# Value products one slot later, in front of a 512-column query product, and key fetches a pair ahead

## The chip, the cores and the metric

The kernel runs on one core of a Trainium2 chip. The metric is the device time of one execution in microseconds. The comparison of interest is between the kernel before the change and the kernel after it.

The engines are called by the names of the profile: PE is TensorE (matmuls), PEld its weight loads, DVE is VectorE, ACT is ScalarE, POOL is GpSimd, and SP is SyncE, which issues nearly all DMAs here. Each engine runs its instructions in the order in which the program gives them.

## The reference

The input is 16 sequences of 256 positions with 256 features. Two layers are computed, each as `x = x + s * silu(f)`, where `s` and `f` both read the layer norm `xn` of `x`. In layer 0 `s` is a linear recurrence and `f` a feed-forward block. The change lies in layer 1, where `s` is causal attention with 16 heads over a compressed key and value of 64 features, and `f` a linear layer with low-rank experts:

```python
q = concat([q_nope, apply_rope(q_rope)])            # per head 128 + 64
c_kv = rms_norm(x @ Wkv_a[:, :64]) * kv_norm_w      # 64 features, shared by the heads
k, v = from c_kv @ Wkv_b ; k gets the rotated shared 64 features as well
scores = where(causal, q @ k.T / sqrt(192), -inf)   # 256 x 256 per head and sequence
out = softmax(scores) @ v @ Wo
```

## The kernel before, in words

The 4096 tokens are worked on in 8 chunks of 512 tokens, that is of two sequences ("batches" b = 0 and 1 of the chunk). Layer 0 fills the first 283 us or so. After that comes the main loop of layer 1, written out by hand: 64 units, with loop variable `i`. A unit is one batch of one group of four heads in one chunk: `ch, r = divmod(i, 8)`, so a chunk has eight slots r = 0 to 7, and b is 0 in even slots and 1 in odd ones. Units 2n and 2n+1 form pair n, which has one chunk and one group of four heads. There are 32 pairs.

All engines are wrapped by a helper (`InOrder`, line 53) that ties each instruction to the one before it on its engine, so the program's order is the order on each engine, and nearly every line of the profile shows L53. Instructions are therefore told apart by their tiles.

What a slot `i` of the loop does, in the order on TensorE:

- `score_pack(u, 0)`: scores (`sc`) of the blocks with 256 and 224 keys. Behind it VectorE adds the mask and takes the maxima (`nm`), ScalarE takes the exponentials into `pr` and sums them (`sr`).
- `query_mm`: a product of 512 columns (`pq`) for the queries of a later pair, number 3 in an even slot, number 0 in an odd slot.
- `score_pack(u, 1)`: the blocks with 192, 160 and 128 keys.
- in an odd slot `query_mm(n, 1)`, another `pq`, and on VectorE `query_mul` (`qmul`).
- `turn(w, ...)` and `send(w)` for the unit before, `w`: VectorE transposes the normalised `pr` in 32x32 blocks into `turned`, and four DMAs on SyncE write it to a DRAM buffer `far`.
- in an even slot from the sixth on, `values_of(n)` for the pair that ended two slots earlier: 16 products of 64x64 weights, seen as 32 records, from `pT` into two PSUM banks `av`, and two copies on ScalarE to `attT`.
- `score_pack(u, 2)`: the blocks with 96, 64 and 32 keys; in an odd slot then `query_mm(n, 2)`, the second `query_mul`, and on GpSimd `query_rot`, which writes `qrot`.
- extra work of the chunk in certain slots: the gate in r = 0 and 1, the transposes `tp` of the next chunk's `xn` in r = 2 (`transpose_chunk`; `xn` is written by VectorE in the same slot, `norm_end`), the keys in r = 4, the router in r = 6, and the output product (`fast_end`) in r = 3, 4, 5 and 7.

`values_of(n)` reads two tiles, `pT[0]` and `pT[1]`, one for each half of the keys. Each has 128 partitions, 64 for each batch. They are filled by `fetch(n, y, b)`: one DMA on SyncE from `far[b]` into `pT[y]`, 384 KB. So a pair needs four fetches, and the products run through the first key half before the second:

```python
for z in (0, 2, 1, 3):
    ...
    heads = q.pT[z % 2][:, :, c0 : c0 + S - n0].rearrange("p (a hh) q -> p a hh q", hh=2)
```

The ring of `pT` has three buffers, that of `far` two, the small PSUM ring (tag `m1`: `pq`, `av`, `tp`, `pg`, `pkv` and others) five, the ring of `sc` three. In an even slot SyncE also issues `query_move`: eight DMAs from `qrot` into `qg`, the queries of a later pair.

The order of fetches before: in even slot 2n+2 `fetch(n, 0, 0)` at the start and `fetch(n, 1, 0)` behind `send`; in odd slot 2n+3 `fetch(n, 0, 1)` and `fetch(n, 1, 1)`, both at the start.

Of the kernel before, what the change touches and what calls it, by code (L numbers as in the profile page):

```python
# [41 lines left out]
def tile_two_layers(ctx: ExitStack, tc: tile.TileContext, d: dict, out: bass.AP):  # L42
# [181 lines left out]
    def m1(name, shape):  # L224
        return place["pool"].tile(shape, F32, tag=place["tag"], name=name)
# [204 lines left out]
    def query_move(n):  # L430
        q = groups[n]
        for r in range(2):
            for h in range(G):
                sp.dma_start(
                    q.qg[64 + 32 * r : 96 + 32 * r, :, h, :],
                    q.rot[32 * h : 32 * h + 32, r, :].rearrange("p (a q) -> p a q", q=32),
                )
# [892 lines left out]
    def gate_end(ch, jp):  # L1330
        k = chunks[ch]
        g = k.g2[:, 2 * jp : 2 * jp + 2, :]
        ve.scalar_tensor_tensor(g, g, 1.0, k.h, ALU.add, ALU.mult)
# [31 lines left out]
    def score_pack(u, pi):  # L1365
        k, b, pack = chunks[u.ch], u.b, PACK[pi]
        if pi == 0:
            u.nm = sm1.tile([P, NQ], F32, tag="nm", name=f"nm_{u.n}", bufs=3)
            u.sr = sm1.tile([P, NQ], F32, tag="sr", name=f"sr_{u.n}", bufs=3)
        qg = groups[u.i // 2].qg  # L1370
        sc = ps_sc.tile([P, CH], F32, tag="sc", name=f"sc_{u.n}_{pi}")
        for a, o in pack:
            pe.matmul(
                sc[:, o : o + 32 * (a + 1)], qg[:, b * NQ + a, :, :].rearrange("p h q -> p (h q)"),
                k.kT[:, b * S : b * S + 32 * (a + 1)], start=True, stop=True,
            )
        ends = [o + 32 * (a + 1) for a, o in pack]
        step = ends[1] - ends[0]
        n = len(pack)
        assert ends == [ends[0] + step * z for z in range(n)]  # L1380
        if ends[0] - 32 + step * n <= CH:
            diag = sc[:, ends[0] - 32 : ends[0] - 32 + step * n].rearrange("p (n s) -> p n s", n=n)[:, :, 0:32]
        else:
            diag = sc[:, ends[0] - step : ends[-1]].rearrange("p (n s) -> p n s", n=n)[:, :, step - 32 : step]
        ve.tensor_tensor(diag, diag, bc(kmask, n), ALU.add)
        for a, o in pack:
            ve.tensor_reduce(
                u.nm[:, a : a + 1], sc[:, o : o + 32 * (a + 1)], AX.X, ALU.max, negate=True
            )
        for a, o in pack:  # L1390
            w = 32 * (a + 1)
            ac.activation(
                u.pr[:, OFF[a] : OFF[a] + w], sc[:, o : o + w], AF.Exp,
                bias=u.nm[:, a : a + 1], accum_out=u.sr[:, a : a + 1],
            )

    def normalise(u, packs):
        blocks = [a for pi in packs for a, _ in PACK[pi]]
        lo, hi = min(blocks), max(blocks) + 1
        ve.reciprocal(u.sr[:, lo:hi], u.sr[:, lo:hi])  # L1400
        for a in blocks:
            v = u.pr[:, OFF[a] : OFF[a] + 32 * (a + 1)]
            gp.tensor_scalar(v, v, u.sr[:, a : a + 1], 1.0, ALU.mult, ALU.mult)
# [32 lines left out]
    def fetch(n, y, b):  # L1436

        q = groups[n]
        if y == b == 0:
            q.pT = {}  # L1440
        if b == 0:
            q.pT[y] = pp.tile([P, G, 3 * P], F32, tag="pT", name=f"pT_{n}_{y}", bufs=3)
        sp.dma_start(
            q.pT[y][64 * b : 64 * b + 64].rearrange("p h q -> p (h q)"),
            q.far[b].rearrange("(y k) s h z q -> y (k s) (h z q)", y=2)[y],
        )
# [35 lines left out]
    def values_of(n):  # L1482

        q = groups[n]
        ch, g = divmod(n, NG)
        k = chunks[ch]
        av = [m1(f"av_{ch}_{g}_{b}", [P, 2, S]) for b in range(2)]
        for z in (0, 2, 1, 3):
            n0 = 64 * z
            c0 = (0, 64, S, S + 64)[z]  # L1490
            heads = q.pT[z % 2][:, :, c0 : c0 + S - n0].rearrange("p (a hh) q -> p a hh q", hh=2)
            for b in range(2):
                rows = slice(64 * b, 64 * b + 64)
                for hh in range(2):
                    pe.matmul(
                        av[b][64 * hh : 64 * hh + 64, :, n0:S], k.rowv[rows, z, :],
                        heads[rows, :, hh, :], start=(z == 0), stop=(z == 3),
                    )
        k.attT.append(a2.tile([P, 2, CH], F32, tag="attT", name=f"attT_{ch}_{g}", bufs=6))
        for b in range(2):  # L1500
            ac.copy(k.attT[g][:, :, b * S : (b + 1) * S], av[b])
# [27 lines left out]
    def out_weights(i):  # L1529
        if i == PER:  # L1530
            gp.tensor_tensor(TO[1], wo(0, 1), wo(0, 0), ALU.subtract)
            gp.tensor_tensor(TO[2], wo(1, 1), TO[1], ALU.subtract)
        elif i == PER + 2:
            gp.tensor_tensor(TO[4], TO[2], wo(1, 0), ALU.subtract)
        elif i == PER + 4:
            gp.tensor_tensor(TO[3], wo(1, 1), wo(0, 1), ALU.subtract)
        elif i == 2 * PER + 1:
            TO[4] = X[0].rearrange("p j (n s) -> p (j n) s", s=DH)[:, 0:KP]
            gp.tensor_tensor(TO[4], TO[2], wo(1, 0), ALU.subtract)
# [105 lines left out]
    for i in range(LAST):  # L1645
        ch, r = divmod(i, PER)
        odd = i % 2 == 1
        u, w = units[i], units[i - 1] if i else None
        here = w is not None and w.i >= LAST - 2
        n = (i + 3) // 2 if odd else (i + 2) // 2  # L1650
        n = n if n < len(groups) else None
        more = ch + 1 < NCH
        last = ch - 1 if ch == NCH - 1 and r in FINISH else None
        fast = ch - 1 if 0 < ch < NCH - 1 else None

        if not odd and n is not None:
            query_move(n)
        if odd and i > 2:
            fetch((i - 3) // 2, 0, 1)
            fetch((i - 3) // 2, 1, 1)  # L1660
        elif i and not odd:
            fetch((i - 2) // 2, 0, 0)
        score_pack(u, 0)
        if w:
            normalise(w, (2,))
        if fast is not None and r > 3:
            fast_begin(fast, r)
        if ch > 1 and r == 0:
            fast_begin(ch - 2, 0)
        out_weights(i)  # L1670
        if r == 1:
            gate_end(ch, 0)
        if r == 2:
            gate_end(ch, 1)
            if more and ch:
                norm_end(ch + 1)
        if r == 5 and more:
            kv_end(ch + 1)
        if i == LAST - 1:

            finish_mm(last, 3, 0, NPAIR)
            finish_out(last, 3)
            last = None
        if w:
            for z in (1, 2):
                turn_here(w, z) if here else turn(w, z)

        if r == 0:
            mid_chunk(ch)
        if r == 7 and more:  # L1690
            key_chunk(ch + 1)
        if n is not None:
            query_mm(n, 0 if odd else 3)
            if not odd:
                query_lat(n, 3)
        if i == 5:
            values_of(0)
        score_pack(u, 1)

        if odd and n is not None:  # L1700
            query_mm(n, 1)
            query_mul(n, 0)
        if w:
            if here:
                turn_here(w, 0)
            else:
                turn(w, 0)
                send(w)
        if not odd:
            if i > 4:  # L1710
                values_of((i - 4) // 2)
            if i:
                fetch((i - 2) // 2, 1, 0)
        score_pack(u, 2)
        normalise(u, (0, 1))

        if odd and n is not None:
            query_mm(n, 2)
            query_mul(n, 1)
            query_rot(n)  # L1720
            query_lat(n, 2)
        if r < 2:
            gate_begin(ch, r)
        if r == 0 and more and ch:
            norm_begin(ch + 1)
        if r == 2 and more:
            transpose_chunk(ch + 1)
        if r == 4 and more:
            kv_begin(ch + 1)
        if r == 6 and more:  # L1730
            router_chunk(ch + 1)
        if last is not None:
            j = FINISH.index(r)
            finish_mm(last, j, 0, NPAIR)
            finish_out(last, j)
        if fast is not None and r in FINISH:
            fast_end(fast, r)
# [94 lines left out]
```

## Time and profile before

| | |
|---|---|
| median of 3 runs | 909.54 us (907.01 to 910.27) |
| profiled execution | 908.09 us, span 906.3 us |
| granted TensorE clock, mean | 0.996 |
| TensorE busy | 894.5 us (99%), 5426 matmuls |
| VectorE, GpSimd, ScalarE busy | 664.7 us (73%), 570.2 us (63%), 475.3 us (52%) |
| value products `av` | 992 records, 80.2 us busy |
| score products `sc` | 1024 records, 175.2 us busy |
| query products `pq` | 512 records, 122.6 + 120.2 us busy |
| fetches `pT<-far` | 124 DMAs of 384 KB, median 4.9 us to landing |
| sends `far<-turned` | 248 DMAs of 192 KB, median 4.3 us to landing |
| moves `qg<-qrot` | 256 DMAs of 64 KB, median 2.8 us to landing |

The span is the time from the first to the last recorded instruction. Busy times add up the records of an engine and count overlapping time once. A matmul's record overlaps with its neighbours, as matmuls are pipelined, so the distance from one start to the next says more than a record's duration. In a timeline, records of the same shape that follow each other are joined, and the first column is the start of the first in microseconds from the start of the span. A bracket names the wait ahead of a record and what ended it.

### The profile page before, as it was taken

The numbers are of one execution on the slowest core, as the hardware profiler recorded it, in microseconds if no ns is written. First come the engines' busy times: TensorE is split into PE (matmuls) and PEld (weight loads), VectorE is DVE, ScalarE is ACT, GpSimd is POOL, SyncE is SP. The second block draws the span as 40 slices with busy tenths as digits, with TensorE's granted clock in tenths as the row PEclk, the third lists the DMA queues.
The fourth block names the chain that finished last, engine by engine and source line by source line (L and its number), as shares of the span: only waits on it lengthen the run. The fifth ranks groups of instructions, "written<-read, shape, count | busy, mean of one in ns | idle before, by whom it ended". The sixth has DMA issues, their size and how long they took to land.

```text
span 906.3 us, 17455 instructions
## 1 busy us (share of the span) xinstructions
PE 894.5 (99%) x5426; PEld 670.2 (74%) x5426; DVE 664.7 (73%) x2017; ACT 475.3 (52%) x1562; POOL 570.2 (63%) x885
## 2 busy tenths in 40 slices
PE   8999999999999999999999999999999999999998
PEld 7768899987767656777677677767767776776776
DVE  6876687665587879668967876896787689678662
ACT  3235556564336646555554664555466456546541
POOL 1228787878345537687586768648776864876541
PEclk9999999999999999999999999999999999999999
DMA  9730000000013887877987887788788778878881
GB/s 282 237 116 2 1 2 1 1 1 2 0 24 75 201 226 172 216 175 180 226 195 176 195 205 178 181 223 209 163 215 189 178 185 224 205 163 219 192 246 35
DMA packets 197404, 134.00 MB, mean 148 GB/s; under 512 B 143104, under 2 KB 187968, under 8 KB 197312
## 3 DMA queue, kind: packets, MB, share of 16 engines
q1 hardware_dynamic: 195184, 128.69, 57.7%
q0 software_dynamic: 1152, 3.67, 1.2%
q8 instruction: 44, 0.72, 0.3%
q10 hardware_dynamic: 976, 0.53, 0.2%
q14 instruction: 48, 0.39, 0.1%
HBM read 63.11 MB, written 52.95 MB: 128 GB/s over the span
## 4 chain that ended last, share of the span: by engine, by line
PE 89%; DMA 4%; SPq 3%; DVE 2%; POOL 1%; issue 0%; ACT 0%; POOLq 0%; ACTq 0%
PE pq L53 21%; PE sc L53 14%; PE po L53 10%; PE av L53 7%; PE r L53 7%; PE f L53 7%; PE ph L53 5%; PE pf L53 5%; PE pg L53 4%; SPq L53 3%; DMA far<-turned 2%; PE pm L53 2%; DMA pT<-far 2%; PE tp L53 2%; PE pkv L53 1%; PE py L53 1%
## 5 line engine op out<-in xcount | busy, mean ns | idle before, releaser
L53 POOL TENSOR_SCALAR pr<-pr,sr 128x256 f32<-128x256 f32 (+7 forms) x512 | 191.6, 393 | 186.7 <-DVE sr L53 181.2
L53 ACT ACTIVATE pr<-sc,nm 128x256 f32<-128x256 f32 (+7 forms) x512 | 189.8, 381 | 218.8 <-DVE sr L53 140.8
L53 PEld LDWEIGHTS sc<-kT,qg 128*128 128x128 f32 x1024 | 157.5, 190 | 54.5 <-issue 40.7
L53 PE MATMUL sc<-kT,qg 128*128 128x256 f32 (+7 forms) x1024 | 175.2, 305 | 0.0
L53 DVE TENSOR_REDUCE nm<-sc 128x1 f32<-128x256 f32 (+7 forms) x512 | 127.6, 301 | 6.6
L53 DVE STREAM_TRANSPOSE turned<-pr 128x512 f32<-128x512 f32 x186 | 123.2, 687 | 10.9 <-POOL pr L53 10.1
L53 PE MATMUL pq<-xnT,wlat 128*128 128x512 f32 x256 | 122.6, 602 | 0.0
L53 PE MATMUL pq<-xnT,wrope 128*128 128x512 f32 x256 | 120.2, 593 | 0.0
L53 ACT ACTIVATION_READ_ACCUMULATOR pr<-sc,nm 128x1 f32 x512 | 104.1, 203 | 0.0
L53 DVE TENSOR_TENSOR sc<-sc,kmask 128x96 f32<-128x96 f32 (+1 forms) x192 | 45.4, 236 | 54.9 <-PE sc L53 53.6
L53 POOL TENSOR_TENSOR qrot<-qmul,qmul 128x512 f32<-128x512 f32 x64 | 83.4, 1323 | 2.8 <-DVE qmul L53 2.8
L53 PE MATMUL av<-pT,rowv 64*64 64x512 f32 (+2 forms) x992 | 80.2, 442 | 4.0 <-DMA pT<-far 3.6
L53 DVE TENSOR_TENSOR qmul<-pq,rot_q 128x512 f32<-128x512 f32 x128 | 80.7, 672 | 0.1
L53 ACT ACTIVATE qg<-pq 64x512 f32<-64x512 f32 x128 | 75.4, 589 | 4.3 <-PE pq L53 3.5
L53 PEld LDWEIGHTS av<-pT,rowv 64*64 64x64 f32 x992 | 37.5, 134 | 43.8 <-issue 31.7
L53 PEld LDWEIGHTS pq<-xnT,wrope 128*128 128x128 f32 x256 | 45.7, 191 | 32.4 <-issue 32.1
L53 PEld LDWEIGHTS pq<-xnT,wlat 128*128 128x128 f32 x256 | 45.7, 191 | 31.6 <-issue 31.6
L53 PEld LDWEIGHTS po<-wout,attT 128*128 128x128 f32 x416 | 58.4, 191 | 9.4 <-issue 4.0
L53 PE MATMUL po<-wout,attT 128*128 128x128 f32 (+1 forms) x416 | 64.2, 308 | 0.0
L53 POOL TENSOR_TENSOR rs<-ve,mhalf 128x4 f32<-128x4 f32 (+1 forms) x17 | 16.8, 986 | 48.6 <-DVE ve L53 34.6
L53 PE MATMUL ph<-xnT,p1T 128*128 128x256 f32 (+1 forms) x128 | 44.3, 503 | 0.8 <-DVE xnT L53 0.8
L53 POOL TENSOR_TENSOR attT<-attT,attT 128x512 f32<-128x512 f32 x36 | 45.1, 1273 | 0.0
(229 smaller groups left out, 1518.7 us busy)
## 6 DMA issues: line engine op xcount, KB each, us to landing
far<-turned SPq DMA_DIRECT2D x248, 192.0 KB, 4.3
pT<-far SPq DMA_DIRECT2D x124, 384.0 KB, 4.9
qg<-qrot SPq DMA_DIRECT2D x256, 64.0 KB, 2.8
x<-in_x_dram SPq DMA_DIRECT2D x7, 512.0 KB, 9.2
out_dram<-x POOLq DMA_DIRECT2D x12, 256.0 KB, 3.5
wqn_wo<-in_wq_nopeT_dram SPq DMA_DIRECT2D x4, 512.0 KB, 4.7
wqn_wo<-in_Wo_dram SPq DMA_DIRECT2D x4, 512.0 KB, 5.7
p2T<-in_proj2T_dram SPq DMA_DIRECT2D x2, 512.0 KB, 8.3
```

What stands on the lines that cost most here:

```text
L53: r = getattr(self.engine, name)(*args, **kw)
```

## The change

The products of pair n move from even slot 2n+4, behind `send` and ahead of `score_pack(u, 2)`, to odd slot 2n+5, behind `score_pack(u, 1)` and ahead of `query_mm(n, 1)`. Pair 0, which was in slot 5 ahead of `score_pack(u, 1)`, is now behind it. The two fetches of the second key half both go into odd slot 2n+3, behind `send` of unit 2n+2. The first fetch of the first half stays at the start of the even slot and the second at the start of the odd slot. The products of the last two pairs, after the loop, keep their place. Every instruction of before is still there, with the same shape.

```diff
         if odd and i > 2:
             fetch((i - 3) // 2, 0, 1)
-            fetch((i - 3) // 2, 1, 1)
         elif i and not odd:
             fetch((i - 2) // 2, 0, 0)
         score_pack(u, 0)
...
-        if i == 5:
-            values_of(0)
         score_pack(u, 1)
 
+        if odd and i > 4:
+            values_of((i - 5) // 2)
         if odd and n is not None:
             query_mm(n, 1)
             query_mul(n, 0)
...
                 turn(w, 0)
                 send(w)
-        if not odd:
-            if i > 4:
-                values_of((i - 4) // 2)
-            if i:
-                fetch((i - 2) // 2, 1, 0)
+        if odd and i > 2:
+            fetch((i - 3) // 2, 1, 0)
+            fetch((i - 3) // 2, 1, 1)
         score_pack(u, 2)
         normalise(u, (0, 1))
```

In the even slots TensorE's order becomes pack 0, `pq`, pack 1, pack 2, extra work. In the odd slots it becomes pack 0, `pq`, pack 1, the products, `pq`, pack 2, `pq`, extra work. ScalarE's two copies to `attT` move with the products.

## The prediction

> **What bounds the kernel now.** I read the profile page first: engine totals, the 40 slices, the chain that ended last, the groups.
>
> ```profile
> PE 894.5 (99%) x5426; PEld 670.2 (74%) x5426; DVE 664.7 (73%) x2017; ACT 475.3 (52%) x1562; POOL 570.2 (63%) x885
> PE   8999999999999999999999999999999999999998
> PE 89%; DMA 4%; SPq 3%; DVE 2%; POOL 1%; issue 0%; ACT 0%; POOLq 0%; ACTq 0%
> L53 PE MATMUL av<-pT,rowv 64*64 64x512 f32 (+2 forms) x992 | 80.2, 442 | 4.0 <-DMA pT<-far 3.6
> ```
>
> TensorE is busy 894.5 of 906.3 us and carries 89% of the chain. No time comes from less work here, since the change issues the same instructions. It can come from three places: TensorE's waits, the order in which its matmuls pipeline, and waits that the new order makes. The fourth line is the moved work, the value products `av`; DMAs hold them up. Next the waits of TensorE and of SyncE's queue:
>
> ```profile
> PE av L53 <- DMA pT<-far: 3.6, 2, 2.2
> PE tp L53 <- DVE xn L53: 1.6, 1, 1.6
> SPq L53 <- DMA far<-turned: 82.0, 64, 4.1
> ```
>
> Third column group: microseconds in all, times, longest. The first row is what the change can remove, the second is a wait it can multiply, the third says that SyncE itself stands 64 times waiting for `far` to land before it may fetch. Now the timeline of TensorE, at the second pair of units (a stalled group of products) and in chunk 3, slots r=2 and r=3 (an ordinary one); the columns are start, duration, instruction, count:
>
> ```profile
> 320.43 1.08 PE L53 MATMUL av<-pT,rowv 64*64 64x512 f32 x4
> 323.66 3.71 PE L53 MATMUL av<-pT,rowv 64*64 64x512 f32 x28 [2.15 <-DMA pT<-far]
> 327.30 0.85 PE L53 MATMUL sc<-kT,qg 128*128 128x96 f32 x6
> ...
> 519.83 0.98 PE L53 MATMUL sc<-kT,qg 128*128 128x192 f32 x6
> 520.74 2.38 PE L53 MATMUL av<-pT,rowv 64*64 64x512 f32 x32
> 523.06 0.85 PE L53 MATMUL sc<-kT,qg 128*128 128x96 f32 x6
> 523.75 1.07 PE L53 MATMUL tp<-ident,xn 128*128 128x128 f32 x8
> 524.65 0.98 PE L53 MATMUL sc<-kT,qg 128*128 128x256 f32 x4
> 525.47 1.88 PE L53 MATMUL pq<-xnT,wrope 128*128 128x512 f32 x4
> 527.18 0.98 PE L53 MATMUL sc<-kT,qg 128*128 128x192 f32 x6
> 528.00 1.88 PE L53 MATMUL pq<-xnT,wrope 128*128 128x512 f32 x4
> ```
>
> An ordinary group takes 523.06 − 520.74 = 2.32 us from its first start to the next group's. The stalled one takes 327.30 − 320.43 = 6.87: it starts, does four products, waits for `pT`.
>
> **The change, part by part.** The sum is made in the profiled execution: 908.09 us, span 906.3. It lies 1.45 below the median 909.54 of the runs; I subtract the same microseconds from the median.
>
> *1. Waits before the products go.* Group lengths beyond 2.31 us: pair 1 6.87 (+4.56), pair 2 2.78 (+0.46), pair 3 3.88 (+1.56): 6.58 us in all. Every later group up to pair 28 is undisturbed. Now each group starts a slot later, about 6 us on, and its second half of `pT` about 1 us after that. Of pair 1 the two last fetches were issued at 319.44–320.53 and landed by 325.37. In the new order they stand behind the four `far` DMAs (320.63–323.56), so I expect them to be issued at about 323 and to land between 327.5 and 328.9; the products would want them at about 328.0. That leaves 0 to 2 us, I take 0.6. Term: −6.0.
>
> *2. Order on TensorE.* Even slots lose a group between score pack 1 and pack 2. With the group, pack 1's start to the end of pack 2 is 523.75 − 519.83 = 3.92. Without it the two packs run as one, as other even slots show:
>
> ```profile
> 303.75 1.57 PE L53 MATMUL sc<-kT,qg 128*128 128x192 f32 x12
> 305.16 2.03 PE L53 MATMUL pkv<-wkva,xnT 128*128 128x128 f32 x16
> ```
>
> That is 1.41: −2.51 a slot. Odd slots had pack 1 straight before the query product, 528.00 − 527.18 = 0.82. Now it is 0.91 (pack 1 to `av`, from 519.83 and 520.74) + 2.32 = 3.23: +2.41. Net −0.10 a pair. Pairs 1 to 27 have that query product behind them, so −2.7. Pairs 28 and 29 stand in front of pack 2 as before, net zero; pair 0 changes places inside its slot, nothing. The step from `av` to `pq` is in no row. The nearest is `av` to `sc`, 0.20 from last start to next, which is inside the 2.32. The other end is one exposed weight load, 0.19, each time: +5.1, so this term lies between −2.7 and +2.4. I take the near row.
>
> [...]
>
> *3. Even slots are 2.5 us shorter for VectorE and GpSimd.* This is the main cost. In r=2 of chunks 1 to 6 the transposes `tp` need `xn`, which VectorE writes after all else. VectorE and GpSimd in that slot:
>
> ```profile
> 519.30 0.87 DVE L53 SCALAR_TENSOR_TENSOR g<-g,h 128x512 f32<-128x512 f32 x1
> 520.10 2.36 DVE L53 TENSOR_SCALAR xn<-x,mv,rs 128x256 f32<-128x256 f32 x4
> 522.38 1.29 DVE L53 STREAM_TRANSPOSE turned<-pr 128x512 f32<-128x512 f32 x2
> 518.36 2.95 POOL L53 TENSOR_TENSOR qrot<-qmul,qmul 128x512 f32<-128x512 f32 x2
> ```
>
> With the slot's start T = 517.30, `xn` ends at T+5.16 (522.46). `tp` starts at T+6.45 and wants its last `xn` 0.36 later; 2.51 earlier that is T+4.30. If VectorE kept its times, `tp` would wait 0.86. The chain behind it on VectorE (two `turned`, mask, maxima), then ScalarE's exponentials, ends at T+8.67 and gates pack 1 of r=3, now wanted at 527.18 − 517.30 − 2.51 = T+7.37. So 1.3 us, with 0.1 to 0.2 for the release 1.5, in six chunks 9.0.
>
> VectorE does not keep its times, I think. It is late in r=2 because it ran without a gap from 511.42. After the change the odd slot r=1 holds 2.3 us of products, in which VectorE catches up: the reciprocal of 516.10 can come at about 513.7, `qmul` ends at about 515.0 rather than 517.4, and `qrot` on GpSimd at about 518.3 rather than 521.31. Then no `qrot` runs beside `xn`. Of the four `xn` the first took 1.36 us (beside a `qrot` of 1.72, which elsewhere takes 1.27), the others 0.40 to 0.43. So `xn` would take 1.4 from about 519.9 and end at T+3.97, in time for `tp`. The exponentials then end at about T+7.5, where pack 1 of r=3 wants T+7.37: with the release 0.2 to 0.45 a chunk. Term: +2.0 (1.3 to 2.7). [...]
>
> *4. Fetches.* The same four DMAs a pair go through SyncE. The first half keeps its issue; the two of the second half come behind `send` in the odd slot, all of them. They still wait for the buffer that half of the same slot's products release (three `pT` buffers), as before; behind them on SyncE stand the eight `qg` moves of the next slot, needed a slot later. The fetch of (second half, first batch) no longer fills time in which SyncE waits for `far`: about +0.5 us a cycle of 17.5 to 18.3 us against 16.7 to 22.9 of TensorE. It costs nothing while TensorE is the slower, and part 1's 0.6 holds the early pairs.
>
> *5. The tail.* Pair 29 waited 2.81 (5.12 − 2.31) in slot 62; in slot 63 it does not. But the last `send` and `fetch` still run after each other on SyncE up to 886.35, the products of pair 30 (884.44, 3.19 long) wait for that, and the time saved ahead is given back there. Between −2.8 and +1.5; I take 0.
>
> ScalarE's `attT` copies (needed 6 us later or more), `mT`, the gate and the router cover their shift with 2 us or more of room; if that cover were gone, each 2.5 us shift would appear once a chunk.
>
> Sum: −6.0 − 2.7 + 2.0 = −6.7. Span 899.6, profiled execution 901.4, median 902.8.
>
> **The rivals.**
> *(a) VectorE does not catch up.* Part 3 costs 9.0: −8.7 + 9.0 = +0.3, so 909.8. For it: VectorE is busy 73% and gapless in r=1 and r=2. Against it: the products give it 2.3 us of cover one slot ahead.
> *(b) Slower: `xn` collides with both `qrot`.* If `qrot` slips a little rather than coming earlier, a second `xn` runs beside it, 1.36 − 0.41 = 0.95 more. Then 1.5 + 0.95 in six chunks is 14.7, −8.7 + 14.7 = +6.0: 915.5. It decides as soon as r=2 loses more than 8.7 / 6 = 1.45 us a chunk. For it: the first `xn` shows the collision. Against: `qmul` would have to come later than now.
> *(c) The fetches only move their wait.* If the second half lands 2 us or more after each early group wants it, about 5 of the 6.58 us stay: −1.6 − 2.7 + 2.0 = −2.3, 907.2. For it: SyncE stands 82 us waiting for `far`, and the fetches now queue behind four more DMAs. Against: a slot is 6 us, a landing 4.9.
> *(d) Larger gain.* No new waits of VectorE, none left early, and the tail keeps its 2.8: −6.6 − 2.7 − 2.8 = −12.1, 897.4.
>
> **How the numbers follow.** Forecast 0.52, (a) 0.13, (b) 0.12, (c) 0.12, (d) 0.11. Half a per cent, 4.5 us, is about what a measurement can tell from no change: 905.0 and 914.1. Faster holds (d) and the forecast less a tenth of it (an exposed weight load, +5.1, puts it at 907.9): 0.11 + 0.47 = 0.58. Same holds that tenth, (a) and (c): 0.05 + 0.13 + 0.12 = 0.30. Slower is (b), 0.12. The range goes from (d) to beyond (a): 897 to 911, leaving (b) out.
>
> **What would show it.** In the profile after: no `av` row with a wait in pairs 1 to 3; `av` to `pq` 2.3 us; packs 1 and 2 of even slots in 1.41; `tp` in r=2 without a wait on `xn`, and `qrot` ended before `xn` starts; a wait of `sc` below 0.5 us in r=3. The prediction is wrong if `tp` or `sc` waits over 1.4 us in each chunk, if `av` still waits for `pT` in the first chunks, or if `av` to `pq` takes 2.5.

## The result and the profile after

The changed kernel takes 922.3 us (median of 5 runs, 919.88 to 923.67) against 907.59 us before (5 runs, 906.49 to 910.27). The ratio is 1.0135, 95% interval 1.0105 to 1.0165: slower by 14.7 us between the medians and by about 12 by the ratio, where 6.7 less was forecast. The profiled execution took 922.3 us with a span of 920.5 us, 14.2 more than before. The engine totals, the chain and the value products on the page of the changed kernel:

```profile
PE 903.8 (98%) x5426; PEld 672.1 (73%) x5426; DVE 666.9 (72%) x2017; ACT 475.8 (52%) x1562; POOL 569.1 (62%) x885
PE 86%; DVE 6%; DMA 5%; ACT 2%; issue 1%; SPq 1%; POOL 0%; DVEq 0%; ACTq 0%; POOLq 0%
L53 PE MATMUL av<-pT,rowv 64*64 64x512 f32 (+1 forms) x992 | 79.6, 439 | 5.1 <-DMA pT<-far 5.1
```

The same 5426 matmuls keep TensorE busy 9.3 us longer, so a large part of the loss shows as records that ran longer, not as waits between them: a lower clock, records that reach into a wait, and a slower step from `av` to `pq`, all seen below. The products still wait for `pT`, 5.1 us instead of 3.6. TensorE's waits, in microseconds, times, longest:

```profile
PE av L53 <- DMA pT<-far: 5.1, 8, 0.9
PE tp L53 <- DVE xn L53: 2.1, 2, 1.6
PE pt L53 <- POOL pr L53: 1.6, 1, 1.6
...
PE sc L53 <- ACT pr L53: 1.0, 2, 0.8
```

I located the 14.2 us by the start of each slot, that is the first 256-column `sc` matmul of its pack 0 on TensorE's timeline. Slots are numbered 0 to 63.

| stretch | before, us | after, us | difference | forecast |
|---|---|---|---|---|
| up to slot 6 | 316.99 | 318.11 | +1.1 | 0 |
| slots 6 to 11 | 60.82 | 64.30 | +3.5 | −6.0 and the order |
| slots 12 to 61 | 488.40 | 492.90 | +4.5 | −2.7 + 2.0 less the first slots' share |
| slot 62 to the end | 40.09 | 45.19 | +5.1 | 0 |

The first row is not the change's: it is there at slot 0 already (271.15 and 272.27), behind the same instructions, and in the profiled executions of the runs below slot 0 starts between 0.3 us earlier and 1.3 us later than in the kernel before. In the third row nearly every even slot is 2.51 us shorter, nearly every odd one 2.51 longer, and two kinds of slots are longer still: r=3 of chunks 2 to 6 by 0.29 more, r=7 of chunks 1 to 6 by 0.50.

One profile of each kernel does not fix the second row. In the four other profiles with the changed order in these slots (runs 4, 5, 6 and 12 below) they take 0.8 to 4.4 more than the 60.82; in the three others with the order of before (runs 7, 10 and 11) 0.5 less to 2.3 more. A gain of 6 is in none.

The products of pairs 1 and 2, on TensorE's timeline of the changed kernel:

```profile
327.86 1.65 PE L53 MATMUL av<-pT,rowv 64*64 64x512 f32 x16
330.21 0.86 PE L53 MATMUL av<-pT,rowv 64*64 64x384 f32 x4 [0.71 <-DMA pT<-far]
331.98 1.08 PE L53 MATMUL av<-pT,rowv 64*64 64x384 f32 x12 [0.90 <-DMA pT<-far]
...
347.68 1.52 PE L53 MATMUL av<-pT,rowv 64*64 64x512 f32 x16
349.91 0.86 PE L53 MATMUL av<-pT,rowv 64*64 64x384 f32 x4 [0.71 <-DMA pT<-far]
351.67 1.93 PE L53 MATMUL av<-pT,rowv 64*64 64x384 f32 x12 [0.90 <-DMA pT<-far]
353.54 3.78 PE L53 MATMUL pq<-xnT,wrope 128*128 128x512 f32 x4
```

Sixteen products of the first key half run through. Then each batch of the second half is waited for by itself. Of pair 2 those two fetches were issued at 344.19 to 345.70 and landed by 351.63, while the products wanted them from 349.2 on. From the first product to the next `pq`, pair 1 takes 5.13 us and pair 2 5.86, where an undisturbed group takes 2.31. The last line is the second loss: four query products that take 1.98 us behind pair 1 take 3.78 here. The windows of the same profile show why; behind the four engines' busy times stands the granted clock, third from the end:

```profile
347.00:351.00 4.00, 3.06 (x26) 1.26 (x24) 3.90 (x15) 0.99 (x4) 2.77 (x6) 1.00 1.14 219
351.00:353.50 2.50, 1.83 (x12) 0.76 (x12) 2.12 (x5) 1.48 (x7) 0.00 (x0) 0.65 0.90 104
353.50:357.00 3.50, 3.50 (x6) 1.51 (x5) 0.00 (x0) 0.83 (x2) 0.00 (x0) 0.50 0.82 174
```

After the two waits TensorE had half its clock for 6.8 us, from 351.75 to 358.58; the first and the last of the three windows hold only a part of that and show a mean. From 351 to 360 that is 2.5 × 0.35 + 3.5 × 0.50 + 3.0 × 0.26 = 3.4 us of lost clock, more than the 1.6 us that the page counts as waits. It is not all extra: in the profile before, one such stretch of 3.41 us lies at the wait of pair 1 (322.99 to 326.40).

### The profile page after: what moved, and what is told of

Read it like the earlier page. It is cut to its first block, busy times and chain, and to the rows that moved or that the text cites. A ratio compares the mean times of both kernels' runs of the same rounds, so it can differ in the third digit from the quotient of the medians.

```text
span 920.5 us, 17381 instructions
## 1 busy us (share of the span) xinstructions
PE 903.8 (98%) x5426; PEld 672.1 (73%) x5426; DVE 666.9 (72%) x2017; ACT 475.8 (52%) x1562; POOL 569.1 (62%) x885
## 4 chain that ended last, share of the span: by engine, by line
PE 86%; DVE 6%; DMA 5%; ACT 2%; issue 1%; SPq 1%; POOL 0%; DVEq 0%; ACTq 0%; POOLq 0%
PE pq L53 22%; PE sc L53 13%; PE po L53 10%; PE r L53 7%; PE f L53 7%; PE av L53 6%; PE ph L53 5%; PE pg L53 5%; PE pf L53 5%; DMA pT<-far 2%; DMA far<-turned 2%; ACT pr L53 2%; PE pkv L53 2%; PE tp L53 2%; DVE nm L53 1%; DVE eq L53 1%
## 5 line engine op out<-in xcount | busy, mean ns | idle before, releaser
L53 POOL TENSOR_SCALAR pr<-pr,sr 128x256 f32<-128x256 f32 (+7 forms) x512 | 193.7, 397 | 202.1 <-DVE sr L53 168.3
L53 PE MATMUL sc<-kT,qg 128*128 128x256 f32 (+7 forms) x1024 | 169.6, 304 | 1.1 <-ACT pr L53 1.0
L53 PE MATMUL pq<-xnT,wrope 128*128 128x512 f32 x256 | 124.8, 612 | 0.0
L53 PE MATMUL av<-pT,rowv 64*64 64x512 f32 (+1 forms) x992 | 79.6, 439 | 5.1 <-DMA pT<-far 5.1
L53 POOL TENSOR_TENSOR qrot<-qmul,qmul 128x512 f32<-128x512 f32 x64 | 80.6, 1279 | 2.8 <-DVE qmul L53 2.8
L53 PEld LDWEIGHTS av<-pT,rowv 64*64 64x64 f32 x992 | 36.2, 133 | 44.8 <-issue 27.9
```

What stands on the lines that cost most here:

```text
L53: r = getattr(self.engine, name)(*args, **kw)
```

## The experiments

Theory Q says that the new order of fetches makes SyncE's chain of moves, sends and fetches longer, and that the products wait for it. Its rival V says that the products' new place costs, on TensorE, VectorE or the PSUM ring.

**1. The fetches alone.** The changed order of fetches, the products in the even slots:

```diff
-            fetch((i - 3) // 2, 1, 1)      # start of the odd slot
...
                 values_of((i - 4) // 2)    # even slot, as before
-            if i:
-                fetch((i - 2) // 2, 1, 0)
+        if odd and i > 2:
+            fetch((i - 3) // 2, 1, 0)
+            fetch((i - 3) // 2, 1, 1)
```

> The products stay in the even slots, only the two fetches of the second key half move behind send in the odd slot. Theory Q (SyncE's queue): the new order makes SyncE's cycle of a pair 18.5 us instead of 16.9, and the products want the second half a slot earlier than in the changed kernel, so av waits for pT in more pairs: 915 to 935 us. Rival V (the loss comes from the products' new place, on TensorE, VectorE and the PSUM ring): the fetch order alone does nothing, 904 to 910.

Measured: 1019.2 us, ratio 1.1187 (1.1143 to 1.1231). Far beyond the range that either theory gave (915 to 935 was Q's), and on the side of Q. TensorE's waits in it:

```profile
PE av L53 <- DMA pT<-far: 55.7, 38, 4.1
```

Most pairs wait, and the mean granted clock is 0.958. So the later fetches need the later products. It does not follow that the two together are free. The other half, later products with the fetches of before, was not run: by the program, with three `pT` buffers the fetch of a second half takes the buffer that the products ahead of it release, so SyncE would stand there until those products, a slot later.

**2. Fetches ahead of `send`.** The changed kernel, with the two second-half fetches ahead of the four `far` DMAs:

```diff
             values_of((i - 5) // 2)
+        if odd and i > 2:
+            fetch((i - 3) // 2, 1, 0)
+            fetch((i - 3) // 2, 1, 1)
...
                 send(w)
-        if odd and i > 2:
-            fetch((i - 3) // 2, 1, 0)
-            fetch((i - 3) // 2, 1, 1)
```

> The products stay in the odd slots, the two second-half fetches go ahead of send (behind them four far DMAs, then the eight qg moves). Theory Q: the second half is issued 2.6 us sooner and SyncE waits once less beside nothing to do; the waits of av in chunks 0 and 1 and most of the tail's loss go: 908 to 915 us, eight qg moves back from 7.2 to about 6.2 us. Rival V: 920 to 924, as the products have not moved.

Measured: 918.28 us, ratio 1.0084 (1.0053 to 1.0114), span 915.9, between the two ranges. Q for the first slots: 6 to 11 take 1.9 us less than before instead of 3.5 more, and pairs 1 and 2 have no wait of the size seen above. The eight `qg` moves of pairs 13 to 27 are issued in 5.9 us on average, 7.5 in the changed kernel and 6.3 before. The middle, slots 12 to 61, still loses 4.5, and from slot 62 on it loses 7.2 us, so Q as I had put it is not enough for the tail.

**3. Fetches on ScalarE's queue.** The changed kernel, with the second half issued by ScalarE at the same place:

```diff
-        sp.dma_start(
+        (ac if y else sp).dma_start(
             q.pT[y][64 * b : 64 * b + 64].rearrange("p h q -> p (h q)"),
```

> The changed kernel with the two second-half fetches issued by ScalarE at the same place of the program; SyncE issues two DMAs less a pair. Theory Q: SyncE's cycle is some 2 us shorter, nothing of av waits for pT in chunks 0 and 1 and the tail loses its 5.1: 908 to 914 us. Rival V: 920 to 924.

Measured: 918.54 us, ratio 1.0105 (1.0069 to 1.0140), again between the two. The first slots gain as in experiment 2 and the `qg` moves take 6.2 us. The tail's loss stays, 7.0 us from slot 62. Taking two issues off SyncE does not help there. The last `far` DMA of each four, from 835 us on, lands up to 6.0 us after its issuing instruction ended, against at most 3.5 before, with fetches from the other queue under way at the same time. In experiment 2, with the same fetches on SyncE's own queue ahead of `far`, it is up to 6.2. That the transfers are in each other's way fits both; it was not tested apart.

**4. Pair 29 back in slot 62.**

```diff
-        if odd and i > 4:
+        if odd and 4 < i < LAST - 1:
             values_of((i - 5) // 2)
...
+        if i == LAST - 2:
+            values_of((i - 4) // 2)
```

> The changed kernel with the products of pair 29 back in slot 62, behind send. Theory Q: the tail's loss of 5.1 is SyncE being late, so the products of pair 29 only wait longer in slot 62, and the sum stays within 1.5 us of the changed kernel: 920 to 924. Rival V: slot 63 is the wrong place for them, 3 to 5 us come back: 916 to 919.

Measured: 926.37 us, ratio 1.0175 (1.0140 to 1.0211). Above both ranges, and far from V's 916 to 919: the products wait up to 5.3 us in slot 62. (Against the changed kernel the intervals of the ratios overlap.) So the new place of pair 29 is not what costs; its fetches are late.

**5. The keys one slot earlier.** The changed kernel with `key_chunk` in r=6.

```diff
-        if r == 7 and more:
+        if r == 6 and more:
             key_chunk(ch + 1)
```

> The changed kernel with key_chunk (transposes pk and ScalarE's kT copy) moved from slot r=7 to r=6. Theory R (the five-bank PSUM ring: in r=7 pk, two query products and two av fill it, and the third query product waits for the copy of pk): of the 0.50 us that each r=7 slot takes more than its 2.51, 0.4 goes; seven chunks, 2.4 to 2.8 us less, 918.5 to 921. Rival (the 0.50 is TensorE's pipelining after the value products): the same time as the changed kernel, 921 to 924.

Measured: 922.37 us, ratio 1.0157 (1.0124 to 1.0189): no gain, and inside the rival's range. Slot r=7 got 0.40 shorter and r=6 0.44 longer, which is the four transposes themselves. The wait stayed in r=7 and changed its owner, on TensorE's timeline of chunk 3:

```profile
577.15 1.96 PE L53 MATMUL pq<-xnT,wlat 128*128 128x512 f32 x4
579.41 2.02 PE L53 MATMUL po<-wout,attT 128*128 128x128 f32 x16 [0.30 <-DVE qmul L53]
```

In the changed kernel it was the third `pq` that started 0.25 late (579.50), when ScalarE's copy of `pk` had just ended (579.46) and freed its bank; now `po` waits for the `qmul` that frees a `pq` bank. In r=7 of the changed kernel `pk`, the first `pq`, two `av` and the second `pq` fill the ring's five banks ahead of the third `pq`. My expectation that the 0.50 would go with `pk` was wrong. That the ring is the cause is argued from this count and from the two releasers; a sixth bank was not tried.

**6. The order of before from pair 25 on**, and **7. the order of before up to pair 4.** Both use the same two switches. `later(n)` says which pairs have their products in the odd slot, and a pair's second half is fetched in the old way where the pair ahead of it has its products in the old place:

```diff
+    def later(n):
+        return 0 <= n < 25          # run 7: 5 <= n < 99
+    def old_fetch(n):
+        return n == 0 and not later(0) or n > 0 and not later(n - 1)
```

> The changed kernel up to pair 24; from pair 25 on (slot 54) products and fetches stand in the order of before. Theory Q (the end of the loop is set by SyncE's chain of moves, sends and fetches, 46.6 us long before and 50.5 after): the tail's 5 us come back, 916 to 919 us. Rival (the end only passes on how late the loop is): no gain, 920 to 924.

> The order of before for pairs 0 to 4 (fetches to pair 5), the changed order from pair 5 on (slot 15). Theory Q: the changed order's waits for pT in chunks 0 and 1 cost more than those that it removes; undone, 2.5 to 4 us come back: 918 to 920. The forecast's own view: these slots gained 6 us, so undoing it costs 6: 926 to 930.

Measured: 920.47 us, ratio 1.0128 (1.0095 to 1.0161), and 919.53 us, ratio 1.0124 (1.0092 to 1.0156). Neither can be told from the changed kernel: the ratios are 0.0007 and 0.0011 lower, well inside the intervals. Run 6 lies in its rival's range, not Q's. Its profile shows the tail no better from slot 62 on, as the products of pair 29 take 6.2 us more than the undisturbed 2.31 there. These two alone did not settle the tail. For run 7, the gain that the forecast saw in the first slots is refuted: undoing it should have cost 6 us, and all six runs lie below 926.

**8. Three at once:** fetches ahead of `send`, keys in r=6, the order of before from pair 25 on.

> Fetches of the second half ahead of send, key_chunk in r=6, and the order of before from pair 25 on. If the three losses add up: 918.3 of the run with fetches ahead, less 2.6 for the ring, less 7 for the tail: 906 to 911, so no better than before. If they share one cause: 914 to 919.

Measured: 913.58 us (12 runs), ratio 1.0058 (1.0036 to 1.0080). Between 911 and 914, the nearer ends of the two expectations: of the changed kernel's 1.35% 0.77 are undone, 7.0 us. What stays is in the middle: its profile still has slots 12 to 61 longer by 4.8, mostly in r=3, r=6 and r=7.

**9 to 11. One part of the loop at a time**, the order of before elsewhere: pairs 0 to 4 with the fetches ahead of `send`, pairs 5 to 24 as in the changed kernel, and pairs from 25 on as in the changed kernel.

```diff
-        return 0 <= n < 25
+        return 0 <= n < 5      # run 9, fetches ahead of send
+        return 5 <= n < 25     # run 10
+        return 25 <= n < 99    # run 11
```

> The changed order for pairs 0 to 4 alone, with the second-half fetches ahead of send; from pair 5 on the order of before. If the gain that the forecast saw is there once the fetches do not stand behind send: the slots to 14 lose 2 to 3 us against before, and the rest is as before: 904 to 908. Rival (no part of the move gains): 909 to 913.

> The changed order for pairs 5 to 24 alone, before's ahead and behind. Theory (the middle costs by itself, 0.29 in each r=3 slot and 0.50 in each r=7 slot, and the order on TensorE gives nothing): +4 us, 911 to 914. The forecast's step 2 and 3 (−0.10 a pair and 0.3 in r=3): −0.5, 907 to 909.

> The changed order from pair 25 on alone. Theory Q (in the tail the fetches behind send lengthen SyncE's chain to the last products): +4 to +7 us, 912 to 917. Rival (the tail's loss only appears after the earlier ones): 907 to 910.

Measured, 12 runs each, with 29 runs of the kernel before on the same chip (910.74 us):

| part changed | us | ratio | 95% interval |
|---|---|---|---|
| pairs 0 to 4, fetches ahead | 908.04 | 0.9969 | 0.9947 to 0.9990 |
| pairs 5 to 24 | 914.93 | 1.0043 | 1.0019 to 1.0066 |
| pairs 25 to 29 | 916.30 | 1.0065 | 1.0040 to 1.0091 |

Run 9 beats both kernels by a little. Run 10 costs 3.9 us, and its profile puts 4.0 us between slots 14 and 53, all in r=3 and r=7. (That profile is of a run 1.8 above the median, and has 3.2 more from slot 62 on, where its order is that of before.) Run 11 costs 5.9 us by itself, inside Q's range and against the rival that it only appears behind other losses. Taken off the 1.35% of the whole change, 0.43% and 0.65% leave 0.27%, 2.4 us, for the first pairs. The three intervals together are wider than that, so these pairs may as well cost nothing; what they do not do is gain 6 us.

Run 11 shows the tail's mechanism. Its last products and what follows, on TensorE's timeline:

```profile
885.53 1.07 PE L53 MATMUL av<-pT,rowv 64*64 64x512 f32 x4
888.19 5.25 PE L53 MATMUL av<-pT,rowv 64*64 64x512 f32 x28 [1.58 <-DMA pT<-far]
893.37 1.97 PE L53 MATMUL pt<-ident,pr 128*128 128x128 f32 x8
```

and its windows, granted clock again third from the end:

```profile
888.00:891.00 3.00, 2.81 (x16) 0.99 (x16) 0.00 (x0) 0.00 (x0) 0.00 (x0) 0.68 0.69 150
891.00:894.00 3.00, 2.91 (x17) 1.40 (x16) 0.00 (x0) 0.91 (x2) 0.00 (x0) 0.50 0.00 0
```

I then took one length from every trace: from SyncE's first `qg` move of slot 58 to the landing of the last fetch, which the products of pair 30 need. It is one chain of issues and of waits for `far` to land. In the changed kernel it is what ended last: of the chain between 866 and 903 us, landings of `far` hold 35.6%, landings of `pT` 17.9%, SyncE's issuing 14.7%. TensorE's wait of 1.58 us for `pr` comes from it too, as VectorE had stood 1.51 us for `far` to land. From the last landing to the end it is 20.0 us before and 19.8 after, in the other runs 19.7 to 25.1.

| order of fetches in the tail | runs | length, us |
|---|---|---|
| as before | before, 6, 8, 9, 10 | 51.3 to 53.0 |
| changed, in any of its forms | after, 1, 2, 3, 4, 5, 7, 11, 12 | 55.3 to 58.4 |

The two groups do not overlap. (The plain time from slot 62 to the end does, a little: 39.9 to 44.8 with the order of before, 44.1 to 50.0 otherwise, as it also holds how late the chain began and the clock.) Run 1 stands in the second row with its products in their old place, so the length goes with the order of the fetches. The rows of SyncE's issues show where it comes from, first in the kernel before, then in the changed one:

```profile
834.63 7.02 SPq L53 DMA_DIRECT2D qg<-qrot  x8
852.70 6.24 SPq L53 DMA_DIRECT2D qg<-qrot  x8
877.43 3.81 SPq L53 DMA_DIRECT2D pT<-far  x3
```

```profile
844.23 8.83 SPq L53 DMA_DIRECT2D qg<-qrot  x8
864.78 7.24 SPq L53 DMA_DIRECT2D qg<-qrot  x8
893.02 1.73 SPq L53 DMA_DIRECT2D pT<-far  x3
```

Before, one fetch of the second half is issued while SyncE would wait for `far` to land anyway (877.43, landing of `far` at 880.13), and two remain behind it. After, three remain (893.02 to 894.75, `far` landed at 893.01). Behind the two fetches the next moves are issued more slowly too: eight `qg` take 8.83 and 7.24 us in slots 58 and 60, before 7.02 and 6.24. Run 2 has the long chain without fetches behind `send`; there `far` lands late, as experiment 3 says.

**12. `xn` a slot earlier.** The changed kernel with `norm_end` in r=1.

```diff
         if r == 1:
             gate_end(ch, 0)
+            if more and ch:
+                norm_end(ch + 1)
```

> The changed kernel with norm_end in slot r=1 instead of r=2. If the 0.29 of each r=3 slot is the exponentials behind xn on VectorE, slot r=3 of chunks 2 to 6 takes 13.53 instead of 13.82, 1.7 us in all. If VectorE is simply behind from r=1 on, it stays 13.82.

Measured: 924.39 us, with 2 runs not to be told from the changed kernel; it was made for slot r=3. Beyond the 2.51 of the products that slot lost 0.29 in each of chunks 2 to 6. With `xn` early it loses 0.03, 0.47, 0.15, 0.00 and 0.00. In three of five chunks the 0.29 is gone with the earlier `xn` and in one it is halved, so it is the work behind `xn`, where nothing else is late. The 0.47 of chunk 3 I cannot explain; run 6, with `xn` in its old place, also has more in chunks 3 and 4 (0.96 and 0.60).

## Why the prediction was wrong

**Step 1 failed.** It left 0.6 us of the 6.58 that the groups of pairs 1 to 3 lost before. Measured, pairs 1 and 2 take 2.82 and 3.55 us more than 2.31 and pair 3 nothing more, so 6.37 stay, and the clock lost behind pair 2 adds 2.5 (half of the time from 353.54 to 358.58). The profile after runs 1.1 us later from slot 0 on. With that taken off, the `far` DMAs stand nearly where the step put them (321.1 to 323.7), but the two fetches of pair 1 took from 323.8 to 325.6 to be issued and landed at 329.1 and 330.8, not at 327.5 and 328.9: 5.3 and 6.4 us behind their issue instead of 4.5 and 5.9. Pair 2, whose fetches stand behind four `far` DMAs in the same way, got no price of its own; the step did not run the queue forward to it. In place of −6.0 the slots 6 to 11 show +3.5 in this profile. Experiment 2 shows that the products' later place is worth about 2 us there if the fetches go ahead of `send`. Without the −6.0 the forecast would be −0.7; the loss itself comes from the steps that follow.

**Step 4 had the size wrong.** It priced the fetches at +0.5 us a cycle. Between slots 58 and 60, where SyncE pauses only for landings, its cycle is 18.07 before (834.63 to 852.70) and 20.55 after (844.23 to 864.78): +2.5, against 17.43 of TensorE for the same two slots. The term left out is the eight `qg` moves behind the two fetches: 8.83 instead of 7.02 in this cycle, 7.5 instead of 6.3 in the middle of the loop. I had named them as queued behind, and priced that at nothing. "It costs nothing while TensorE is the slower" did not cover this place: SyncE was the slower one already in the kernel before, and the step's own range for TensorE began at 16.7.

**Step 5 follows from it.** "I take 0" became +5.1 in this profile, and run 11 has 5.9 for the tail alone. The chain from `send` to `fetch` that the step named is the right bound; it did not stay as long as it was, from the moves of slot 58 to the last landing it grew from 51.7 to 56.6 us.

**Step 2 had its bounds right and its value wrong.** The sum of −0.10 a pair became 0.00, as the even slots gave exactly −2.51 and the odd ones +2.51. The step from `av` to `pq` is 0.20, as taken. But the second `pq` product starts 0.53 behind the first instead of 0.43, a tenth of a microsecond that the step did not look for. It lies between the two ends given, 0 and 0.19, the time of one weight load of `pq` in this trace. About half of that shows; whether it is the load is not shown.

**Step 3 was right for what it named and incomplete.** `tp` in r=2 waited in chunk 1 alone (0.5 us). Pack 1 of r=3 waited 0.29 where 0.2 to 0.45 was forecast, and experiment 12 ties it to `xn`. The slots r=7 were missed: 0.50 each, 3.0 us over six chunks, from the PSUM ring. The prediction gave room to the `attT` copies, the gate and the router and did not look at the banks. In r=7 VectorE works on the router until 577.0 (chunk 3), so the scores' maxima, the exponentials and, behind them, ScalarE's copy of `pk` come late.

**The clock was in no step by name.** The waits cost more than the page counts as waits, for two reasons. The records ahead of a wait reach into it: the 16 products of pair 1's first half show 1.65 us, where half of an undisturbed group takes 1.16, and 1.60 us of waits made the group 2.82 longer at a granted clock of 1.00. And at pair 2's second wait the clock fell, 3.4 us in all.

Of the rivals, (c) had the mechanism of the first slots, a wait that moves behind four more DMAs, with a price of −2.3 instead of a loss. It bounded itself to the waits that were there before. The slower rival (b) came nearest, with +6.0, by another mechanism that does not show: in chunks 2 to 6 all four `xn` take 0.39 to 0.44 us, as step 3 expected without a `qrot` beside them, and only in chunk 1 one takes 1.35.

## What to carry to other kernels

When a transfer is moved in a queue that is busy without a break, run the whole queue forward from the point where it first falls behind, and give a price to every DMA that now stands behind the moved one. Here a fetch that sat in another transfer's landing wait (issued at 877.43 us, landing at 880.13) was free, and was not free behind it: SyncE's cycle grew from 18.07 to 20.55 us. Where a ring of banks is full, moving one tenant can move the wait, as in run 5 (922.37 us against 922.3 for the changed kernel); count the allocations between a bank's first use and its release in the busiest slot before adding two.

## What the runs showed of the hardware

The granted TensorE clock fell to 0.50 for 6.8 us (351.75 to 358.58) behind two waits of 0.71 and 0.90 us that lay 1.8 us apart, with TensorE busy 3.06 of the 4 us from 347 to 351. Behind the same two waits of pair 1, 20 us earlier, it stayed at 1.00. So two waits of under 1 us each were enough in one place and not in the other; the longest wait of TensorE in this profile is 1.6 us.

In the profile before, the two stretches at 0.50 that end within the run last 3.41 us each and begin 92 × 3.413 us apart (8.96 and 322.99). In the changed kernel's they last 6.83 and 3.41 us and begin 158 × 3.413 us apart (351.75 and 891.06). On a grid of such steps, both waits of pair 2 fall into one step (348.34 to 351.75), those of pair 1 into two, which fits that the clock fell behind one and not the other. No sharp limit shows: in the changed kernel a step with 1.03 us of idle TensorE was enough (887.64 to 891.05), and one with 1.24 was not (880.82 to 884.23).

The issue of eight equal `qg` moves of 64 KB took 5.3 to 8.8 us in the profiles before and after. On average of pairs 13 to 27 it was 6.3 us before, with `far` sends directly ahead in the queue, and 7.5 after, with two 384 KB fetches ahead; in the other runs 5.9 to 6.4 and 7.3 to 7.8, but for the run of the fetches alone (7.0).

`far` sends landed later with fetches under way: up to 6.0 us after their issue with the fetches on ScalarE's queue and up to 6.2 with them ahead on SyncE's own, against 3.5 before (the last of each four, from 835 us on). The kernel took 918.54 us with the first (run 3) and 918.28 with the second (run 2).
